# Decay weights of a graph layer: a scan along each row replaced by counts in packed bytes

## The chip, the cores and the metric

The kernel runs on one core of a Trainium2 chip. A core has five engines that run side by side and wait for one another through semaphores: TensorE (PE: matrix products, results in the memory PSUM), VectorE (DVE) and ScalarE (ACT: both work element by element on 128 partitions), GpSimd (POOL), and SyncE (SP), which here only issues transfers. Sixteen DMA engines move data between the main memory (HBM) and the core's own memory (SBUF). The metric is the time in microseconds (us) of one execution on the device.

## The reference, cut to what matters

`x` is 4096 x 64, `adj` is a 4096 x 4096 matrix of zeros and ones in fp32 (67.1 MB), and `weight` is 64 x 64.

```python
h = maximum(layernorm(x), 0)
support = h @ weight
mask = (adj != 0)
rank = cumsum(mask, axis=1)
deg = rank[:, -1:]
k = minimum(deg, 100)
pos = rank - (deg - k)
w = mask * where(pos > 0, 0.5 ** (k - pos), 0)
out = x + w @ support + bias
```

For a neighbour `j` of row `i`, let `c` be the number of neighbours of the same row that stand behind `j`. Its weight is 2 to the power of minus `c` if `c` is under 100, and 0 otherwise. A row's last neighbour has weight 1, the one ahead of it 1/2, and so on. So the work has three parts: count, along each row and from its end, the neighbours behind each column; turn the count into a power of two; and multiply the 4096 x 4096 weights by the 4096 x 64 support. TensorE sums over the partitions, so the weights must have the column `j` on the partitions, while `adj` arrives with the row `i` there: somewhere the matrix must be transposed.

## The kernel before

It takes 32 tiles of 128 rows (2 MB each). For each tile DVE makes factors `f` (1/2 at a neighbour, else 1) and runs a scan along the row from the last column to the first, which multiplies the factors up in `S`. The weight of column `j` is `S[j+1] - S[j]`. TensorE takes this difference while it transposes: two matrix products with an identity and a negative identity for each block of 128 columns. ACT copies the transposed weights from PSUM to SBUF as bf16, eight blocks to a copy. Then TensorE multiplies them by the support, which stands in three bf16 parts, 192 columns in all; ACT copies the result out, and POOL adds the three parts and the residual.

```python
apool = ctx.enter_context(tc.tile_pool(name="apool", bufs=3))      # 3 tiles of adj
work = ctx.enter_context(tc.tile_pool(name="work", bufs=2))
ps_t = ctx.enter_context(tc.tile_pool(name="ps_t", bufs=3, space=bass.MemoryType.PSUM))
ps_o = ctx.enter_context(tc.tile_pool(name="ps_o", bufs=2, space=bass.MemoryType.PSUM))
x_sb = const.tile([P, C, D], F32, name="x_sb")
nc.scalar.dma_start(x_sb, x.rearrange("(c p) d -> p c d", p=P))
# ... constants; layernorm on DVE and ACT: mean, xc, sq, var, rstd, hn ...
# ... hn transposed (line 118, fp32), times weight (line 131), cut into 3 bf16 parts: sup ...

def aggregate(po, wT, t, g):
    nonlocal osb
    for k in range(G):                                             # G = 8 blocks
        c = g * G + k
        nc.tensor.matmul(po, wT[:, c, :], sup[:, c].rearrange("p s d -> p (s d)"),   # line 148
                         start=(c == 0), stop=(c == C - 1))
    if g < NG - 1:
        return
    parts = work.tile([P, 3, D], F32, name="parts")
    nc.scalar.activation(parts, po.rearrange("p (s d) -> p s d", d=D), AF.Copy)      # 153
    # ...
    nc.gpsimd.tensor_add(parts[:, 1, :], parts[:, 1, :], parts[:, 2, :])             # 157
    nc.gpsimd.tensor_add(parts[:, 0, :], parts[:, 0, :], parts[:, 1, :])             # 158
    nc.gpsimd.tensor_add(o, parts[:, 0, :], xb[:, t, :])                             # 159
    # ... every fourth tile: nc.gpsimd.dma_start of osb ...

for t in range(C):                                                 # 32 tiles
    a_sb = apool.tile([P, N], F32, name="a_sb")
    nc.sync.dma_start(a_sb, adj[t * P:(t + 1) * P, :])
    f = work.tile([P, N], BF16, name="f")
    nc.vector.tensor_scalar(f, a_sb, 0.0, 0.5, op0=ALU.is_equal, op1=ALU.max)        # 167
    S = S_bufs[t % 2]
    nc.vector.tensor_tensor_scan(S[:, 0:N][:, ::-1], f[:, ::-1],                     # 169
                                 floor_sb.to_broadcast([P, N]), 2.0, op0=ALU.mult, op1=ALU.max)
    wT = work.tile([P, C, P], BF16, name="wT")
    po = ps_o.tile([P, 3 * D], F32, name="po")
    for g in range(NG):                                            # 4 groups of 8 blocks
        pt = ps_t.tile([P, G, P], F32, tag="pt", name=f"pt{t}_{g}")
        for k in range(G):
            j = (g * G + k) * P
            nc.tensor.matmul(pt[:, k, :], S[:, j + 1:j + 1 + P], ident_b, start=True, stop=False)  # 177
            nc.tensor.matmul(pt[:, k, :], S[:, j:j + P], nident_b, start=False, stop=True)         # 178
        nc.scalar.activation(wT[:, g * G:(g + 1) * G, :], pt, AF.Copy)               # 179
        if pending is not None:
            aggregate(*pending)
        pending = (po, wT, t, g)
```

Of the kernel before, what the change touches and what calls it, by code (L numbers as in the profile page):

```python
# [7 lines left out]

F32 = mybir.dt.float32
BF16 = mybir.dt.bfloat16  # L10
AF = mybir.ActivationFunctionType
ALU = mybir.AluOpType
AX = mybir.AxisListType

MAX_NEIGH = 100
EPS = 1e-5


@with_exitstack
def kernel(  # L20
# [5 lines left out]
    bias: bass.AP,  # L26
    out: bass.AP,
):
    """out = x + w @ (relu(layernorm(x)) @ weight) + bias.

    w[i, j] = 2^-c for a neighbour j of row i with c neighbours behind it (in the same row)
    and c < MAX_NEIGH, else 0.

    Decay weights: along each row, from the last column to the first,
        S[j] = max(f[j] * S[j+1], 2^-(MAX_NEIGH-1)),  S[N] = 2,  f = 1/2 at a neighbour, else 1.
    Then w[j] = S[j+1] - S[j]: 2^-c at a neighbour, 0 elsewhere, and 0 once S sits on its floor,
    which it reaches at the MAX_NEIGH-th neighbour from the end. All of S and w are powers of two
    (or 0), so bf16 holds them exactly. The tensor engine takes the difference while it
    transposes: wT = S[:, j+1].T @ I + S[:, j].T @ (-I).

    The fp32 support is split into three bf16 parts that sum to it exactly (8 + 8 + 8
    significant bits), so the aggregation is an fp32 product with fp32 accumulation.
    """
    nc = tc.nc
    P = 128
    N, D = x.shape
    C = N // P
    G = 8
    NG = C // G
    OG = 4  # L50

    const = ctx.enter_context(tc.tile_pool(name="const", bufs=1))
    setup = ctx.enter_context(tc.tile_pool(name="setup", bufs=1))
    apool = ctx.enter_context(tc.tile_pool(name="apool", bufs=3))
    work = ctx.enter_context(tc.tile_pool(name="work", bufs=2))
    ps_t = ctx.enter_context(tc.tile_pool(name="ps_t", bufs=3, space=bass.MemoryType.PSUM))
    ps_o = ctx.enter_context(tc.tile_pool(name="ps_o", bufs=2, space=bass.MemoryType.PSUM))

# [1 line left out]
    x_sb = const.tile([P, C, D], F32, name="x_sb")  # L60
    nc.scalar.dma_start(x_sb, x.rearrange("(c p) d -> p c d", p=P))
    w_sb = const.tile([P, D], F32, name="w_sb")
    for s in range(2):
        nc.scalar.dma_start(w_sb[s * D:(s + 1) * D, :], weight)
    bias_sb = const.tile([P, D], F32, name="bias_sb")
    nc.scalar.dma_start(bias_sb, bias.rearrange("(o d) -> o d", o=1).to_broadcast([P, D]))

# [1 line left out]
    ident = const.tile([P, P], F32, name="ident")  # L69
    make_identity(nc, ident)  # L70
    ident_b = const.tile([P, P], BF16, name="ident_b")
    nc.gpsimd.tensor_copy(ident_b, ident)
    nident_b = const.tile([P, P], BF16, name="nident_b")
    nc.gpsimd.tensor_scalar_mul(nident_b, ident, -1.0)
    floor_sb = const.tile([P, 1], F32, name="floor_sb")
    nc.gpsimd.memset(floor_sb, 2.0 ** -(MAX_NEIGH - 1))
    S_bufs = []
    for b in range(2):
        S = const.tile([P, N + 1], BF16, name=f"S{b}")
        nc.gpsimd.memset(S[:, N:N + 1], 2.0)  # L80
        S_bufs.append(S)

# [1 line left out]
    def rows(t):  # L84
        return t.unsqueeze(2).to_broadcast([P, C, D])

    mean = setup.tile([P, C], F32, name="mean")
    nc.vector.reduce_sum(mean, x_sb, axis=AX.X)  # L88
    nc.vector.tensor_scalar_mul(mean, mean, 1.0 / D)
    xc = setup.tile([P, C, D], F32, name="xc")  # L90
    nc.vector.tensor_sub(xc, x_sb, rows(mean))  # L91
    sq = setup.tile([P, C, D], F32, name="sq")
    nc.scalar.activation(sq, xc, AF.Square)  # L93
    var = setup.tile([P, C], F32, name="var")
    nc.vector.reduce_sum(var, sq, axis=AX.X)
    nc.vector.tensor_scalar(var, var, 1.0 / D, EPS, op0=ALU.mult, op1=ALU.add)
    # 1 / sqrt(var), with a Newton step for the last bits: y * (1.5 - 0.5 * var * y * y)
    rstd = setup.tile([P, C], F32, name="rstd")
    nc.scalar.activation(rstd, var, AF.Sqrt)
    nc.vector.reciprocal(rstd, rstd)  # L100
    corr = setup.tile([P, C], F32, name="corr")
    nc.vector.tensor_mul(corr, var, rstd)
    nc.vector.tensor_mul(corr, corr, rstd)
    nc.vector.tensor_scalar(corr, corr, -0.5, 1.5, op0=ALU.mult, op1=ALU.add)
    nc.vector.tensor_mul(rstd, rstd, corr)
    hn = setup.tile([P, C, D], F32, name="hn")
    nc.vector.tensor_mul(hn, xc, rows(rstd))  # L107

    xb = const.tile([P, C, D], F32, name="xb")
    nc.gpsimd.tensor_add(xb, x_sb, bias_sb.unsqueeze(1).to_broadcast([P, C, D]))  # L110

# [1 line left out]
    hT = setup.tile([P, C // 2, P], F32, name="hT")  # L113
    for g in range(C // 2 // G):
        pt = ps_t.tile([P, G, P], F32, tag="pt", name=f"pth{g}")
        for k in range(G):
            a = g * G + k
            nc.tensor.transpose(pt[:, k, :], hn[:, 2 * a:2 * a + 2, :].rearrange("p c d -> p (c d)"), ident)  # L118
        nc.scalar.activation(hT[:, g * G:(g + 1) * G, :], pt, AF.Relu)  # L119

    sup = const.tile([P, C, 3, D], BF16, name="sup")
    CS = G * P // D
    for g in range(C // CS):
        pt = ps_t.tile([P, G, P], F32, tag="pt", name=f"pts{g}")
        # the two row halves of hT go to one bank each
        pv = pt.rearrange("p (s h) (q d) -> p s (h q) d", s=2, d=D)
        part = sup[:, g * CS:(g + 1) * CS].rearrange("p (k s) e d -> p s k e d", s=2)
        for k in range(CS // 2):
            a = g * (CS // 2) + k
            for s in range(2):  # L130
                nc.tensor.matmul(pv[:, s, k, :], hT[s * D:(s + 1) * D, a, :], w_sb[s * D:(s + 1) * D, :],  # L131
                                 start=True, stop=True)
        rest = setup.tile([P, 2, CS // 2, D], F32, name="rest", bufs=2)
        nc.scalar.activation(part[:, :, :, 0, :], pv, AF.Copy)  # L134
        nc.vector.tensor_sub(rest, pv, part[:, :, :, 0, :])  # L135
        nc.scalar.activation(part[:, :, :, 1, :], rest, AF.Copy)
        nc.vector.tensor_sub(part[:, :, :, 2, :], rest, part[:, :, :, 1, :])

# [1 line left out]
    out_t = out.rearrange("(c p) d -> p c d", p=P)  # L140
    osb = None
    pending = None

    def aggregate(po, wT, t, g):
        nonlocal osb
        for k in range(G):
            c = g * G + k
            nc.tensor.matmul(po, wT[:, c, :], sup[:, c].rearrange("p s d -> p (s d)"),  # L148
                             start=(c == 0), stop=(c == C - 1))
        if g < NG - 1:  # L150
            return
        parts = work.tile([P, 3, D], F32, name="parts")
        nc.scalar.activation(parts, po.rearrange("p (s d) -> p s d", d=D), AF.Copy)  # L153
        if t % OG == 0:
            osb = work.tile([P, OG, D], F32, name="osb")
        o = osb[:, t % OG, :]
        nc.gpsimd.tensor_add(parts[:, 1, :], parts[:, 1, :], parts[:, 2, :])  # L157
        nc.gpsimd.tensor_add(parts[:, 0, :], parts[:, 0, :], parts[:, 1, :])  # L158
        nc.gpsimd.tensor_add(o, parts[:, 0, :], xb[:, t, :])  # L159
        if t % OG == OG - 1:  # L160
            nc.gpsimd.dma_start(out_t[:, t - OG + 1:t + 1, :], osb)  # L161

    for t in range(C):
        a_sb = apool.tile([P, N], F32, name="a_sb")
        nc.sync.dma_start(a_sb, adj[t * P:(t + 1) * P, :])
        f = work.tile([P, N], BF16, name="f")
        nc.vector.tensor_scalar(f, a_sb, 0.0, 0.5, op0=ALU.is_equal, op1=ALU.max)  # L167
        S = S_bufs[t % 2]
        nc.vector.tensor_tensor_scan(S[:, 0:N][:, ::-1], f[:, ::-1], floor_sb.to_broadcast([P, N]), 2.0,  # L169
                                     op0=ALU.mult, op1=ALU.max)  # L170
        wT = work.tile([P, C, P], BF16, name="wT")
        po = ps_o.tile([P, 3 * D], F32, name="po")
        for g in range(NG):
            pt = ps_t.tile([P, G, P], F32, tag="pt", name=f"pt{t}_{g}")
            for k in range(G):
                j = (g * G + k) * P
                nc.tensor.matmul(pt[:, k, :], S[:, j + 1:j + 1 + P], ident_b, start=True, stop=False)  # L177
                nc.tensor.matmul(pt[:, k, :], S[:, j:j + P], nident_b, start=False, stop=True)  # L178
            nc.scalar.activation(wT[:, g * G:(g + 1) * G, :], pt, AF.Copy)  # L179
            if pending is not None:  # L180
                aggregate(*pending)
            pending = (po, wT, t, g)
    aggregate(*pending)


# [26 lines left out]
```

## Time and profile before

| | |
|---|---|
| time, median of 3 runs | 440.5 us (437.2 to 440.66) |
| span of the profiled run | 435.5 us |
| busy: DVE, POOL, PE, ACT | 370.5, 331.3, 255.4, 148.8 us |
| read from HBM | 68.22 MB, a mean of 159 GB/s over the span |
| mean granted TensorE clock | 0.863 of full speed |

Busy times of different engines overlap, so they do not add up to the span. A row of the profile's groups gives the line of the kernel, the engine, the operation, the written and the read tile with their shapes, the count, the busy time, the mean duration of one in ns, and the idle time of the engine just before them with what ended it. The chain of work that ended last is followed back from the last instruction, at each step to what released it; POOL leads it here, and an engine that leads it can itself be held up by another, so it has to be read together with the order of time. In the table of stretches the columns are the stretch in us, its length, the busy time of PE, PEld (the loads of the fixed operand), DVE, ACT and POOL with the number of instructions in brackets, the granted TensorE clock, the busy share of the DMA engines and their GB/s.

### The profile page before, as it was taken

What the parts mean: (1) busy time and instruction counts of PE and PEld (TensorE: products, weight loads), DVE (VectorE), ACT (ScalarE), POOL (GpSimd) and SP (SyncE); (2) the same over time, 40 slices, a digit from 0 to 9 for tenths busy, and PEclk for the clock granted to TensorE, in tenths of its full rate; (3) what the DMA queues carried; (4) which work ended last, traced back from release to release, by engine and by line L of the source; (5) the groups of instructions that cost most, each with busy time, mean ns of one, the idle gap of its engine ahead of it and who ended that gap; (6) DMA issues with size and microseconds to landing.
All of it is one profiled execution on the core that took longest, in us unless ns stands there. A gap on an engine that the chain in (4) does not pass through costs nothing.

```text
span 435.5 us, 6885 instructions
## 1 busy us (share of the span) xinstructions
PE 255.4 (59%) x3152; PEld 245.7 (56%) x3152; DVE 370.5 (85%) x79; ACT 148.8 (34%) x171; POOL 331.3 (76%) x116
## 2 busy tenths in 40 slices
PE   0000029857749666877748549578387569585394
PEld 0000028857639556766648549567387568585383
DVE  0089974999997997999979998999989979999570
ACT  0011107534415405434225314344064036251253
POOL 1040000699999997999999996999999969999752
PEclk9999999988887968888669788987888869698798
DMA  8914850055555555355553455555554553300000
GB/s 322 350 32 170 337 206 36 2 194 194 193 194 206 193 194 190 111 184 196 181 191 148 182 193 206 194 193 194 194 206 172 191 188 102 135 2 2 12 2 12
DMA packets 6365, 69.70 MB, mean 160 GB/s; under 512 B 961, under 2 KB 1985, under 8 KB 2241
## 3 DMA queue, kind: packets, MB, share of 16 engines
q1 hardware_dynamic: 4608, 67.11, 42.1%
q10 hardware_dynamic: 1344, 1.11, 1.1%
q0 software_dynamic: 384, 1.05, 0.7%
q8 instruction: 24, 0.39, 0.4%
q14 instruction: 5, 0.03, 0.0%
HBM read 68.22 MB, written 1.05 MB: 159 GB/s over the span
## 4 chain that ended last, share of the span: by engine, by line
POOL 69%; PE 8%; DVE 7%; issue 5%; DMA 5%; ACT 4%; POOLq 0%; ACTq 0%
POOL osb L159 26%; POOL parts L157 23%; POOL parts L158 20%; DMA x_sb<-in_x_dram 5%; PE po L148 3%; DVE f L167 3%; ACT wT L179 2%; DVE S L169 2%; PE pt L177 2%; PE pt L178 2%; PE pts L131 1%; PE pth L118 1%; ACT parts L153 1%; POOL out_dram L161 1%; DVE hn L107 1%
## 5 line engine op out<-in xcount | busy, mean ns | idle before, releaser
L169 DVE TENSOR_TENSOR_SCAN S<-f,floor_sb 128x4096 bf16<-128x4096 bf16 x32 | 280.9, 8779 | 19.3 <-PE pt L178 19.3
L177 PE MATMUL pt<-ident_b,S 128*128 128x128 bf16 x1024 | 152.9, 242 | 64.8 <-DVE S L169 64.3
L179 ACT ACTIVATE wT<-pt 128x1024 bf16<-128x1024 f32 x128 | 130.1, 1024 | 156.0 <-PE pt L178 156.0
L157 POOL TENSOR_TENSOR parts<-parts 128x64 f32<-128x64 f32 x32 | 114.6, 3581 | 71.0 <-ACT parts L153 70.9
L178 PE MATMUL pt<-nident_b,S 128*128 128x128 bf16 x1024 | 152.4, 241 | 0.0
L177 PEld LDWEIGHTS <-S 128*128 128x128 bf16 x1024 | 112.8, 111 | 69.8 <-DVE S L169 69.5
L148 PE MATMUL po<-sup,wT 128*128 128x192 bf16 x1024 | 124.9, 274 | 46.4 <-ACT wT L179 46.3
L148 PEld LDWEIGHTS <-wT 128*128 128x128 bf16 x1024 | 97.9, 110 | 49.8 <-ACT wT L179 48.0
L159 POOL TENSOR_TENSOR osb<-parts,xb 128x64 f32<-128x64 f32 x32 | 115.0, 3595 | 2.5
L178 PEld LDWEIGHTS <-S 128*128 128x128 bf16 x1024 | 113.0, 110 | 0.8 <-issue 0.6
L158 POOL TENSOR_TENSOR parts<-parts 128x64 f32<-128x64 f32 x32 | 90.1, 2815 | 2.5
L167 DVE TENSOR_SCALAR f<-a_sb 128x4096 bf16<-128x4096 f32 x32 | 76.8, 2402 | 1.0
L118 PE MATMUL pth<-ident,hn 128*128 128x128 f32 x16 | 3.6, 423 | 63.1 <-DVE hn L107 63.1
L118 PEld LDWEIGHTS pth<-ident,hn 128*128 128x128 f32 x16 | 3.3, 227 | 63.0 <-issue 63.0
L153 ACT ACTIVATE parts<-po 128x192 f32<-128x192 f32 x32 | 10.5, 329 | 62.4 <-POOL osb L159 59.6
L88 DVE TENSOR_REDUCE mean<-x_sb 128x32 f32<-128x2048 f32 x1 | 2.3, 2286 | 22.9 <-DMA x_sb<-in_x_dram 22.9
L110 POOL TENSOR_TENSOR xb<-x_sb,bias_sb 128x2048 f32<-128x2048 f32 x1 | 4.5, 4495 | 22.1 <-DMA bias_sb<-in_L_gnn_bias_dram 22.1
L135 DVE TENSOR_TENSOR rest<-pts,sup 128x1024 f32<-128x1024 f32 x2 | 2.5, 1226 | 7.6 <-ACT sup L134 7.6
L93 ACT ACT_TABLE_LOAD x1 | 1.3, 1283 | 21.0 <-issue 21.0
L93 ACT ACTIVATE sq<-xc 128x2048 f32<-128x2048 f32 x1 | 1.9, 1909 | 18.9 <-DVE xc L91 18.9
L161 POOL DMA_DIRECT2D out_dram<-osb x8 | 6.3, 792 | 2.4 <-POOL osb L159 2.4
L119 ACT ACTIVATE hT<-pth 128x1024 f32<-128x1024 f32 x2 | 2.0, 1024 | 8.3 <-PE pth L118 8.3
(28 smaller groups left out, 26.3 us busy)
## 6 DMA issues: line engine op xcount, KB each, us to landing
a_sb<-in_adj_dram SPq DMA_DIRECT2D x32, 2048.0 KB, 8.0
out_dram<-osb POOLq DMA_DIRECT2D x8, 128.0 KB, 6.1
w_sb<-in_L_gnn_weight_dram ACTq DMA_DIRECT2D x2, 16.0 KB, 12.1
bias_sb<-in_L_gnn_bias_dram ACTq DMA_DIRECT2D x1, 32.0 KB, 3.0
x_sb<-in_x_dram ACTq DMA_DIRECT2D x1, 0.2 KB, 22.2
```

The source lines that it names most:

```text
L118: nc.tensor.transpose(pt[:, k, :], hn[:, 2 * a:2 * a + 2, :].rearrange("p c d -> p (c d)"), ident)
L148: nc.tensor.matmul(po, wT[:, c, :], sup[:, c].rearrange("p s d -> p (s d)"), start=(c == 0), stop=(c == C - 1))
L153: nc.scalar.activation(parts, po.rearrange("p (s d) -> p s d", d=D), AF.Copy)
L157: nc.gpsimd.tensor_add(parts[:, 1, :], parts[:, 1, :], parts[:, 2, :])
L158: nc.gpsimd.tensor_add(parts[:, 0, :], parts[:, 0, :], parts[:, 1, :])
L159: nc.gpsimd.tensor_add(o, parts[:, 0, :], xb[:, t, :])
L161: nc.gpsimd.dma_start(out_t[:, t - OG + 1:t + 1, :], osb)
L167: nc.vector.tensor_scalar(f, a_sb, 0.0, 0.5, op0=ALU.is_equal, op1=ALU.max)
L169: nc.vector.tensor_tensor_scan(S[:, 0:N][:, ::-1], f[:, ::-1], floor_sb.to_broadcast([P, N]), 2.0, op0=ALU.mult, op1=ALU.max)
L177: nc.tensor.matmul(pt[:, k, :], S[:, j + 1:j + 1 + P], ident_b, start=True, stop=False)
L178: nc.tensor.matmul(pt[:, k, :], S[:, j:j + P], nident_b, start=False, stop=True)
L179: nc.scalar.activation(wT[:, g * G:(g + 1) * G, :], pt, AF.Copy)
```

## The change

It is a new formulation of the whole kernel. Its steps:

1. Rows are taken in 8 chunks of 512, and columns in 2 halves, the right half first: 16 units, each of 4 loaded tiles of 128 rows x 2048 columns (1 MB). The tile buffers become 8 of 1 MB instead of 3 of 2 MB. Within a unit, partition `p` of a tile holds one of 16 rows that lie next to one another, so a tile's 128 runs of 8 KB lie 256 KB apart in HBM.
2. `convert`: DVE (in three of the 64 tiles ACT, by the sign) writes a byte for each element, 64, or 65 at a neighbour. Four columns, 512 apart, share one 32-bit word.
3. `transpose`: TensorE transposes such words as fp32 numbers, four columns in each pass, 4 blocks to a tile; `settle` (DVE) copies them out. Read as fp16, a word is two numbers, each with two masks in it: a step of its low byte and a step of its high byte are two fixed steps of its value.
4. `totals`, `split`, `suffix`, `clamp`: products with band matrices sum up each run of 32 columns, ACT reads the sums as bytes from PSUM, a product with `later` adds up what lies behind each run, and DVE cuts that at 100.
5. `scan`: for each 128 fp16 numbers, one product with a triangular matrix counts within the runs and a second adds what lies behind. The constants are such that the fp32 sum in PSUM has the two counts in its two lowest bytes.
6. `weigh`: ACT reads those bytes straight from PSUM and writes 2 to the power of minus the count, 128 x 1024 elements to an instruction.
7. `aggregate`: the normalised `x`, in two parts, is the fixed operand, and the weights are streamed 512 at a time. The product with `weight` comes after the sum, once for each chunk (`project`).
8. All these tasks are put in one fixed order by a list in the program, and the engines are held to it. Extra products on an unused tile keep TensorE busy in the first stretch. Two tiles of `adj` are loaded ahead of `x`, and the last chunk is drained, projected and stored in two halves.

What it is for: to take the serial scan off DVE, to transpose four columns with each pass, and to have no engine wait long for another. The core of the diff, cut (the constants, the layernorm and its own transposes are left out, and the list is shortened):

```diff
-    apool = ctx.enter_context(tc.tile_pool(name="apool", bufs=3))
-    work = ctx.enter_context(tc.tile_pool(name="work", bufs=2))
-    ps_t = ctx.enter_context(tc.tile_pool(name="ps_t", bufs=3, space=bass.MemoryType.PSUM))
-    ps_o = ctx.enter_context(tc.tile_pool(name="ps_o", bufs=2, space=bass.MemoryType.PSUM))
+    apool = ctx.enter_context(tc.tile_pool(name="apool", bufs=NA))          # NA = 8
+    bpool = ctx.enter_context(tc.tile_pool(name="bpool", bufs=6))
+    mpool = ctx.enter_context(tc.tile_pool(name="mpool", bufs=3))
+    wpool = ctx.enter_context(tc.tile_pool(name="wpool", bufs=NP + 4))      # NP = 8
+    ps_t = ctx.enter_context(tc.tile_pool(name="ps_t", bufs=2, space=bass.MemoryType.PSUM))
+    ps_v = ctx.enter_context(tc.tile_pool(name="ps_v", bufs=4, space=bass.MemoryType.PSUM))
...
-        nc.vector.tensor_scalar(f, a_sb, 0.0, 0.5, op0=ALU.is_equal, op1=ALU.max)
-        nc.vector.tensor_tensor_scan(S[:, 0:N][:, ::-1], f[:, ::-1], floor_sb.to_broadcast([P, N]), 2.0,
-                                     op0=ALU.mult, op1=ALU.max)
...
+    def convert(n):
+        m8 = bpool.tile([P, Q, E], U8, name="m8")                           # Q = 512, E = 4
+        m_v, a_v = m8.rearrange("p q e -> p e q"), tiles.pop(n).rearrange("p (e q) -> p e q", e=E)
+        if n in signed:                                                     # (4, 8, 11)
+            nc.scalar.activation(m_v.bitcast(I8), a_v, AF.Sign)
+        else:
+            nc.vector.tensor_scalar(m_v, a_v, 0.0, 64.0, op0=ALU.not_equal, op1=ALU.add)
...
+        for c in range(c0, c1):                                             # transpose: 4 to a tile
+            nc.tensor.transpose(pts[u, tt][:, c, :], m32[:, c * P:(c + 1) * P], ident)
...
+            nc.vector.tensor_copy(mw, pt)                                   # settle: 128 x 512 words
...
+        for e in range(E // 2):                                             # totals: 8 to a unit
+            for c in range(CB):
+                nc.tensor.matmul(tot[SUB * c:SUB * (c + 1), :], band[:, at:at + SUB], masks[u][:, c, :, e], ...)
...
+    def split(u):
+        nc.scalar.activation(sums8[u], tots[0].bitcast(U8).rearrange("p (i f) -> p f i", f=4)[:, 1:3, :], AF.Copy)
...
+        for f in range(2):                                                  # suffix
+            nc.tensor.matmul(px, later[:, 1 - u % H, f, :], sums[:, f, :], start=(f == 0), stop=(f == 1))
...
+        nc.vector.tensor_scalar(behind[u], ..., excess[:, h:h + 1], float(MAX_NEIGH), op0=ALU.subtract, op1=ALU.min)
...
+    def scan(u, k):                                                         # 8 to a unit
+        v = vs[u, k] = ps_v.tile([P, W], F32, tag="v", name="v")            # W = 512 rows
+        nc.tensor.matmul(v, tri, masks[u][:, k % CB, :, k // CB], start=True, stop=False)
+        nc.tensor.matmul(v, where[:, k, :], behind[u], start=False, stop=True)
+
+    def weigh(u, k):
+        wts[u, k] = wpool.tile([P, 2, W], F32R, name="wk")
+        v = vs.pop((u, k)).bitcast(U8).rearrange("p (i f) -> p f i", f=4)[:, :2, :]
+        nc.scalar.activation(wts[u, k], v, AF.Exp, scale=-LN2, bias=floor)
+
+    def aggregate(u, k):
...
+        for s in range(2):
+            nc.tensor.matmul(accs[0], hr[:, h * HB + k // CB * 2 * CB + s * CB + k % CB, :, :].rearrange("p s d -> p (s d)"), wk[:, s, :],
+                             start=((h, k, s) == (1, 0, 0)), stop=((h, k, s) == (0, NP - 1, 1)))
...
+    def drain(g, part=None):                                                # ACT; the last half DVE
+    def project(g, part=None):                                              # PE: 4 fp32 products, 64 columns
+    def finish(g, part=None):                                               # DVE add, then the store
...
+    places = {"v": 4, "t": 2, "b": 6, "w": NP + 4}                          # the list: next task by rank
+    while kinds:                                                            # and by when it may start
...
+            if end is not None and at - end > 700:
+                warm((at - end) // 430)                                     # extra products on TensorE
...
+    for i in nc.cur_bb.bb.instructions:                                     # PE, DVE, ACT, POOL:
+            if i.engine in last:                                            # held to program order
+                tc.add_manual_dep(i, last[i.engine], ..., reason="program order")
```

## The prediction, made before the changed kernel ran

> **What bounds the kernel now.** I read the costliest groups first, then the chain that ended last, then the order of time of single engines, then the table of stretches. The groups:
>
> ```profile
> L169 DVE TENSOR_TENSOR_SCAN S<-f,floor_sb 128x4096 bf16<-128x4096 bf16 x32 | 280.9, 8779 | 19.3 <-PE pt L178 19.3
> L179 ACT ACTIVATE wT<-pt 128x1024 bf16<-128x1024 f32 x128 | 130.1, 1024 | 156.0 <-PE pt L178 156.0
> L159 POOL TENSOR_TENSOR osb<-parts,xb 128x64 f32<-128x64 f32 x32 | 115.0, 3595 | 2.5
> L167 DVE TENSOR_SCALAR f<-a_sb 128x4096 bf16<-128x4096 f32 x32 | 76.8, 2402 | 1.0
> ```
>
> DVE needs a scan and a conversion for each tile, 8.78 + 2.40 = 11.2 us, and has almost no idle time ahead of the two (19.3 + 1.0 us in all). The chain gives POOL 69%, but the order of time of POOL shows the same 64-element addition in two durations:
>
> ```profile
> 145.60 8.70 POOL L157 TENSOR_TENSOR parts<-parts 128x64 f32<-128x64 f32 x1
> ...
> 167.82 0.32 POOL L158 TENSOR_TENSOR parts<-parts 128x64 f32<-128x64 f32 x1
> ```
>
> It takes 0.32 us by itself, and 8.7 us while a DVE scan runs (from 145.38, for 8.81 us). POOL is held up by DVE and now and then hands a delay of 2.3 us on. DVE is the bound: 32 x 11.2 = 358 us, 20 us of stalls, about 31 us before the first scan at 31.05 and 13.5 us after the last. That leaves some 13 us of the 435.5 for the layernorm's pieces on DVE. PE idles in each tile, and the stretches show what that costs it and what the transfers can do:
>
> ```profile
> 127.00:128.00 1.00, 0.00 (x0) 0.00 (x0) 1.00 (x1) 0.00 (x0) 1.00 (x1) 1.00 0.69 279
> ...
> 129.00:130.00 1.00, 0.00 (x0) 0.00 (x0) 0.97 (x2) 0.21 (x1) 1.00 (x2) 0.50 0.00 0
> ```
>
> ```profile
> 47.00:55.00 8.00, 0.00 (x0) 0.00 (x0) 8.00 (x2) 0.00 (x0) 0.00 (x0) 1.00 1.01 432
> ...
> 88.00:400.00 312.00, 211.18 (x2579) 203.35 (x2577) 297.37 (x55) 116.54 (x134) 297.60 (x84) 0.83 0.47 172
> ```
>
> PE's last product before the pause starts at 124.12; by 129 the granted clock is half. Transfers reach 432 GB/s where a buffer is free, and 172 on average, as they wait for DVE. Two rows give PE's rate at full and half clock, by the distance of starts (0.05 to 0.06 and 0.10 to 0.11 us for 128 columns):
>
> ```profile
> 122.12 0.22 PE L178 MATMUL pt<-nident_b,S 128*128 128x128 bf16 x1
> 122.17 0.22 PE L177 MATMUL pt<-ident_b,S 128*128 128x128 bf16 x1
> ...
> 132.99 0.31 PE L177 MATMUL pt<-ident_b,S 128*128 128x128 bf16 x1
> 133.09 0.31 PE L178 MATMUL pt<-nident_b,S 128*128 128x128 bf16 x1
> ```
>
> **What the Trainium skill says.** "TensorE: Matmul & The Clock Gate", Part 1: the clock is halved after an idle window of about 3.4 us and given back after as long a busy one. The trace agrees (idle from 124.3, half clock before 129). "ScalarE: Activation LUTs", What ACT_TABLE_LOAD costs: any function costs one element a cycle at 1.2 GHz, a per-partition bias adds about 93 ns, neighbours overlap by as much. The trace has two copies of 128x1024 in 1.93 us at 130.02, so 0.92 us from start to start; no Exp with a bias runs here. "VectorE: DVE Perf Modes", Mode 2x_2P: a tensor-with-scalar operation from SBUF to SBUF handles two fp32 elements a cycle. L167 agrees (4096 in 2.29 us alone, 1787 a microsecond), but no byte output runs here. The first page's Part 3 says that products into different strips of 32 output rows run side by side, 2.38 times as fast for three; no run here shows it.
>
> **The change, part by part.** Removed: all 281 us of scans, half-clock waits, POOL's additions in the loop. Added, engine by engine, over 16 units of 4 MB:
>
> *DMA.* 68.2 MB / 432 GB/s = 158 us, ready at about 161 with the start. The 256 KB distance between runs is new; I assume the same rate.
>
> *DVE.* A conversion has half L167's elements. Of L167's 2.29 us alone, 4096 elements at two a cycle of 0.96 GHz (that page's clock) are 2.13 and 0.16 is fixed; 2048 take 1.07 + 0.16 = 1.23 us, and 61 of them 75 us. Settle copies 512 words from PSUM; L135 does 1024 in 1226 ns, so about 0.65 us, times 64 = 42 us. Clamps 16 x 0.65 = 10. Layernorm and setup about 15. Sum 142 us.
>
> *ACT.* Weigh: 0.92 us, plus 0.09 us for its bias, = 1.01; x 128 = 129 us. Split 16 x 0.92 = 15. Seven drains of 512 elements: 0.92 - 512 x 0.00083 = 0.49, so 3.5. Three conversions at 1.9 (L93's 2048 elements take 1909 ns) = 6. Layernorm pieces and x's own copies about 10, a table load 1.3 (as at L93). Sum 165 us.
>
> *PE* at full clock. 128 columns take 55 ns and eight products of 192 start 0.66 us ahead of the next work, 82 ns each; the slope is 0.42 ns a column, so 512 columns take 0.217 us. Scan and aggregate are four such products for each of the 128 steps: 0.868 x 128 = 111 us. This assumes that the fp32r weights stream at bf16's rate. Transposes: L118 shows 16 fp32 blocks in 3.65 us, 0.228 each, right after 63 us of idle PE. The record there says clock 1.00, but I take it as the half clock by the page above, so 0.114 warm; 256 x 0.114 = 29. Totals 16 x 0.5 (side by side) = 8; suffix 16 x 0.43 = 7; project 8 x 0.9 (fp32, small, estimated from L131's 62 ns for half as deep a product, with a load each) = 7. Sum 162 us, plus extra warming products early, which cost nothing.
>
> So for each unit of 4 tiles DMA needs 9.8 us, PE 10.1, ACT 9.6 and DVE 8.3: four engines nearly equal, where before one had 11.2 us for each half as large a tile (22.4 for the same 4 MB).
>
> *On the path.* Two tiles and x are 3.1 MB, 7.3 us, landed by about 11 us with some 3 us of start and latency (as 2 MB took 7.6 us to land, 4.85 of them at the full rate); tiles three and four land by 16. Then convert 1.2, transpose 0.5, settle 0.65, totals 0.6, split 1.0, suffix 0.45, clamp 0.65, scan 0.45 and about eight hand-overs of 0.15 us: the first weigh at about 23 us. After it ACT still has about 152 us and PE about 157 (a few transposes and one unit's totals are done). The end behind the last weigh: aggregate 0.45, drain 0.4, project 0.5, finish 0.3, store about 3: 5 us. PE: 23 + 157 + 5 = 185; ACT: 180; DMA: 161 + the last unit's chain of 7 us + 8 weighs of 1.01 + 5 = 181. With four streams this close, a fixed order and 2 to 4 buffers between them, none runs without gaps. I add 4% of the 157 us, 6 us: a span of 191. The times before lie 1.7 to 5.2 us above the profiled span, so 193 us for the median.
>
> **The rivals.** (1) *DVE becomes the bound*: if a byte output 4 bytes apart lifts the conversion out of the doubled rate, it takes 2.29 us (as DVE's 2048-element fp32 additions do, L107), DVE has 207 us and the time is near 235. Against it, L167's output is 16-bit beside a 32-bit input and runs doubled, so the output's width alone doesn't stop it. 8%. (2) *The clock falls*: with the mean 0.83 of before PE's 157 us become 189, the time 225. Against it: gaps of over 3.4 us caused that clock, and the new order leaves none in steady flow. A few such gaps would cost 2 us each. 7%. (3) *fp32r at half rate or transposes at 0.228 us*: 55 or 29 us more on PE, 220 to 250. L118 leaves the second open. 8%. (4) *Transfers bound*: at 380 GB/s for scattered runs 68.2 MB take 180 us and the time is 203. The rate of 403 GB/s in the first 11 us of before, with small packets between, speaks against much worse. 20%. (5) *The four fit together almost without gaps*: 184 us. 20%.
>
> **Range and chances.** The centre is 193. Case 5 gives the low end, case 4 and a larger loss by waiting (10% of 157) the high end: 182 to 212. Each of cases 1 to 3 lies above it, though they are the less likely; all of them still lie at half the time before. Slower than 431 us would take an error of two in the bound's sum. So 0.98 for faster.
>
> **What would show each step right or wrong.** Weigh near 1.0 us from start to start, x128, with ACT busy over 80% from 25 us on. Convert near 1230 ns and settle near 650; a mean of 2300 means rival 1. Granted clock over 0.95 after 25 us; 512-column products 0.22 us apart; transposes 0.11 us apart. GB/s near 400 in steady flow, with loads that wait for a free buffer rather than tiles that wait for a load. The first weigh at 22 to 25 us. A tail of 5 us behind the last weigh. The prediction is wrong if one of these unit costs is off by 10%, as that engine then sets the pace for all 16 units.

## The result, and the profile after

The changed kernel takes 210.05 us (median of 5 runs, 209.83 to 211.0) against 440.5 us before: a ratio of 0.479, 95% interval 0.477 to 0.481. The profiled span is 209.0 us. The first lines are the busy time of each engine and the chain that ended last, from the page of the changed kernel:

```profile
PE 194.1 (93%) x1089; PEld 112.6 (54%) x1089; DVE 152.2 (73%) x184; ACT 174.3 (83%) x172; POOL 30.8 (15%) x43
...
DMA 36%; PE 35%; DVE 18%; ACT 4%; POOL 3%; issue 1%; DVEq 0%; POOLq 0%; ACTq 0%
```

Four streams are close to one another, as the change intended, and the chain names two of them, DMA and PE, with equal shares. The groups that took the place of the scan, the transposes and the copies:

```profile
L328 ACT ACTIVATE wk<-v,floor 128x1024 fp32r<-128x1024 uint8 x128 | 139.1, 1118 | 13.8 <-PE v L323 10.7
L273 DVE TENSOR_SCALAR m<-a_sb 128x2048 uint8<-128x2048 f32 x61 | 87.9, 1445 | 12.4 <-DMA a_sb<-in_adj_dram 12.2
L336 PE MATMUL acc<-wk,hr 128*128 128x512 f32 x256 | 91.4, 444 | 1.6 <-DVE hr L262 0.9
L283 PE MATMUL pt<-ident,m 128*128 128x128 f32 x256 | 47.5, 276 | 5.1 <-DVE m L273 4.2
L292 DVE COPY mt<-pt 128x512 uint32<-128x512 uint32 x61 | 41.6, 685 | 13.6 <-PE pt L283 13.4
L322 PE MATMUL v<-mt,tri 128*128 128x512 f16 x128 | 50.7, 396 | 0.4 <-ACT wk L328 0.4
```

The 281 us of scans are gone. No PE group of these has more than 5.1 us of idle time ahead of it, where line 177 (the first product of each transpose) had 64.8 before:

```profile
L177 PE MATMUL pt<-ident_b,S 128*128 128x128 bf16 x1024 | 152.9, 242 | 64.8 <-DVE S L169 64.3 <-DVE rest L135 0.5
```

The stretches (columns as before) show where each engine stands in steady flow, and that the start and the end are different:

```profile
25.00:40.00 15.00, 11.80 (x61) 5.82 (x60) 14.05 (x17) 13.77 (x13) 6.73 (x2) 1.00 1.02 422
...
100.00:120.00 20.00, 19.63 (x115) 10.91 (x113) 17.98 (x20) 17.74 (x18) 1.30 (x2) 1.00 1.01 421
...
180.00:200.00 20.00, 19.87 (x103) 10.94 (x101) 3.51 (x6) 19.20 (x20) 0.56 (x1) 1.00 0.02 7
200.00:209.00 9.00, 4.04 (x14) 2.55 (x14) 0.91 (x3) 2.32 (x3) 0.00 (x0) 0.71 0.05 15
```

In steady flow PE is busy for 98% of the time at full clock, and the transfers run at 421 GB/s without a break. The last load lands at 169.7 us, 39 us ahead of the end. A busy PE can hide waits, since the ends of its products are modelled; so I took the distances from start to start. One step of the changed kernel, from PE's order of time (start, duration, both in us):

```profile
148.03 0.71 PE L336 MATMUL acc<-wk,hr 128*128 128x512 f32 x2
148.58 0.40 PE L322 MATMUL v<-mt,tri 128*128 128x512 f16 x1
148.81 0.38 PE L323 MATMUL v<-behind,where 128*128 128x512 f16 x1
149.03 0.38 PE L283 MATMUL pt<-ident,m 128*128 128x128 f32 x2
149.17 0.71 PE L336 MATMUL acc<-wk,hr 128*128 128x512 f32 x2
```

The aggregate's pair takes 0.55 us, the two scan products 0.23 and 0.22, two transposes 0.14: 1.14 us to the next step. I sorted the distances from 46 to 178 us by the product and its two neighbours; what lies above the lower quartile of each sort comes to some 4.5 of 132 us. So PE works almost without gaps. The instants of the 16 splits give the length of a unit: from the third at 45.7 to the fifteenth at 177.5 us, 10.98 us each, where I had 10.1 for PE without waits. (A split is the one instruction in each unit in which ACT reads the sums of the runs.)

### The profile page after: what moved, and what is told of

The parts are those of the page before. It is cut to its first block, busy times and chain, and to the rows that moved or that the text cites. A ratio compares the mean times of both kernels' runs of the same rounds, so it can differ in the third digit from the quotient of the medians.

```text
span 209.0 us, 2957 instructions
## 1 busy us (share of the span) xinstructions
PE 194.1 (93%) x1089; PEld 112.6 (54%) x1089; DVE 152.2 (73%) x184; ACT 174.3 (83%) x172; POOL 30.8 (15%) x43
## 4 chain that ended last, share of the span: by engine, by line
DMA 36%; PE 35%; DVE 18%; ACT 4%; POOL 3%; issue 1%; DVEq 0%; POOLq 0%; ACTq 0%
DMA a_sb<-in_adj_dram 36%; PE acc L336 12%; DVE m L273 8%; PE v L322 6%; PE v L323 5%; PE pt L283 5%; DVE mt L292 3%; PE po L359 2%; ACT wk L328 2%; PE tot L302 2%; ACT xt L221 2%; POOL rstd L252 2%; PE pc L227 2%; PE ps L313 1%; DVE var L250 1%
## 5 line engine op out<-in xcount | busy, mean ns | idle before, releaser
L328 ACT ACTIVATE wk<-v,floor 128x1024 fp32r<-128x1024 uint8 x128 | 139.1, 1118 | 13.8 <-PE v L323 10.7
L273 DVE TENSOR_SCALAR m<-a_sb 128x2048 uint8<-128x2048 f32 x61 | 87.9, 1445 | 12.4 <-DMA a_sb<-in_adj_dram 12.2
L336 PE MATMUL acc<-wk,hr 128*128 128x512 f32 x256 | 91.4, 444 | 1.6 <-DVE hr L262 0.9
L283 PE MATMUL pt<-ident,m 128*128 128x128 f32 x256 | 47.5, 276 | 5.1 <-DVE m L273 4.2
L292 DVE COPY mt<-pt 128x512 uint32<-128x512 uint32 x61 | 41.6, 685 | 13.6 <-PE pt L283 13.4
L322 PE MATMUL v<-mt,tri 128*128 128x512 f16 x128 | 50.7, 396 | 0.4 <-ACT wk L328 0.4
L283 PEld LDWEIGHTS pt<-ident,m 128*128 128x128 f32 x256 | 34.3, 141 | 29.3 <-issue 5.6
L323 PE MATMUL v<-behind,where 128*128 128x512 f16 x128 | 48.3, 377 | 0.0
L336 PEld LDWEIGHTS acc<-wk,hr 128*128 128x128 f32 x256 | 40.5, 190 | 11.3 <-issue 3.6
L307 ACT ACTIVATE sums<-tot 128x1024 f16<-128x1024 uint8 x16 | 16.5, 1029 | 0.2 <-PE tot L302 0.2
L209 PE MATMUL none<-junk 128*128 128x512 bf16 x31 | 10.8, 492 | 1.3 <-DVE junk L126 1.3
L302 PE MATMUL tot<-mt,band 128*32 128x512 f16 x128 | 10.2, 392 | 1.5 <-DVE mt L292 1.2
L341 POOL TENSOR_TENSOR xr<-xr,bias_sb 128x256 f32<-128x256 f32 x8 | 8.6, 1073 | 10.2 <-DMA bias_sb<-in_L_gnn_bias_dram 10.0
## 6 DMA issues: line engine op xcount, KB each, us to landing
w_sb<-in_L_gnn_weight_dram SPq DMA_DIRECT2D x2, 16.0 KB, 16.5
```

The costliest lines, as they stand in the source:

```text
L273: nc.vector.tensor_scalar(m_v, a_v, 0.0, 64.0, op0=ALU.not_equal, op1=ALU.add)
L283: nc.tensor.transpose(pts[u, tt][:, c, :], m32[:, c * P:(c + 1) * P], ident)
L292: nc.vector.tensor_copy(mw, pt)
L302: nc.tensor.matmul(tot[SUB * c:SUB * (c + 1), :], band[:, at:at + SUB], masks[u][:, c, :, e], start=(h == 1 and e == 0), stop=(e == 1), sk ...
L307: nc.scalar.activation(sums8[u], tots[0].bitcast(U8).rearrange("p (i f) -> p f i", f=4)[:, 1:3, :], AF.Copy)
L322: nc.tensor.matmul(v, tri, masks[u][:, k % CB, :, k // CB], start=True, stop=False)
```

## The experiments

**What sets the pace.** Three kernels each take away part of what one theory holds for the bound: PE's products, ACT's elements, or the loads.

One aggregate product for each step:

```diff
-        for s in range(2):
+        for s in range(1):
             nc.tensor.matmul(accs[0], hr[...], wk[:, s, :],
-                             start=((h, k, s) == (1, 0, 0)), stop=((h, k, s) == (0, NP - 1, 1)))
+                             start=((h, k, s) == (1, 0, 0)), stop=((h, k, s) == (0, NP - 1, 0)))
```

> The aggregate makes one product for each step in place of two (the second half of the weights is computed but left out of the sum, so the output lacks part of the sum). Theory 1, PE sets the pace: a step of 1.147 us loses at least one 512-column product of 0.23 to 0.28 us, PE then needs about 8.7 us for a unit, less than the transfers (10.0) and ACT (9.3), and the time falls from 210 to 187-195 us. Theory 2, ACT sets the pace (busy 174 of 209 us): within 3 us of 210. Theory 3, the transfers set the pace (36% of the chain): within 3 us of 210.

Measured 206.96 us (206.62 to 207.4), so theory 1 as I had put it missed: about 30 us of products (128 at 0.23) were taken away, and 3 us came back.

Half of each weigh:

```diff
-        nc.scalar.activation(wts[u, k], v, AF.Exp, scale=-LN2, bias=floor)
+        nc.scalar.activation(wts[u, k][:, :1, :], v[:, :1, :], AF.Exp, scale=-LN2, bias=floor)
...
-            nc.tensor.matmul(accs[0], hr[...], wk[:, s, :], ...)
+            nc.tensor.matmul(accs[0], hr[...], wk[:, 0, :], ...)
```

> Each weigh handles only the first 512 of its 1024 elements, and both aggregate products stream that half (the second half of the weights is left out, the number of products is unchanged). ACT loses about 128 x 0.43 = 55 us. Theory 1, PE sets the pace: steps stay at 1.147 us and only the last six, where PE waits for ACT, shorten: 204-209 us. Theory 2, ACT sets the pace: under 185 us. Theory 3, transfers: within 3 us of 210.

Measured 208.14 us (208.07 to 208.63). ACT's busy time from 46 to 178 us falls from 120 to 82 us, and PE keeps 131 of 132. ACT does not set the pace, and the step of PE stays at 1.14 to 1.15 us, so the 0.55 of its pair holds no wait for ACT.

Half of the loads:

```diff
+        if n % 2:
+            tiles[n] = pairs[n - 1]
+            return
-        tiles[n] = apool.tile([P, N // H], F32, tag="a_sb", name="a_sb")
+        pairs[n] = tiles[n] = apool.tile([P, N // H], F32, tag="a_sb", name="a_sb")
```

> Every second tile is not loaded: its conversion reads the tile ahead of it again (half of adj is left out; all other work is unchanged). Bytes read fall from 68 to 35 MB. Theory 1, PE sets the pace: 205-210 us, at most the start gets shorter. Theory 3, the transfers set the pace in the middle, as the chain says: under 195 us. Theory 2, ACT: as theory 1.

Measured 211.59 us (211.02 to 211.87): the transfers alone do not set it either, though the chain of the changed kernel gave them 36%. The time lies 1.5 us above the changed kernel and above all three ranges; in the profile the first weigh comes at 28.8 us, 1.3 us later than there (see "The start"). With half of them gone the chain of this kernel reads:

```profile
PE 79%; DVE 11%; POOL 4%; ACT 2%; issue 2%; DVEq 0%; POOLq 0%; ACTq 0%
```

Each wait for a transfer had another stream of nearly the same pace behind it, and the chain can show only one of the two. DVE's order of time in the kernel with one aggregate product shows what holds that one:

```profile
90.21 0.68 DVE L292 COPY mt<-pt 128x512 uint32<-128x512 uint32 x1
91.43 1.38 DVE L273 TENSOR_SCALAR m<-a_sb 128x2048 uint8<-128x2048 f32 x1 [0.54 <-DMA a_sb<-in_adj_dram]
92.70 0.67 DVE L292 COPY mt<-pt 128x512 uint32<-128x512 uint32 x1
93.91 1.39 DVE L273 TENSOR_SCALAR m<-a_sb 128x2048 uint8<-128x2048 f32 x1 [0.54 <-DMA a_sb<-in_adj_dram]
95.19 0.74 DVE L318 TENSOR_SCALAR behind<-ps,excess 128x512 f16<-128x512 f32 x1
```

A conversion starts every 2.49 us, the time of 1 MB at 421 GB/s, and waits for its load. Settles and clamps, whose data are ready, stand behind it in DVE's fixed order, and PE and ACT wait for them. The settle at 90.21, for instance, copies what PE had transposed by 88.9; PE's totals wait for it, and ACT's split for the totals:

```profile
90.94 0.64 PE L302 MATMUL tot<-mt,band 128*32 128x512 f16 x8 [1.34 <-DVE mt L292]
```

```profile
91.62 1.02 ACT L307 ACTIVATE sums<-tot 128x1024 f16<-128x1024 uint8 x1 [0.64 <-PE tot L302]
```

From 46 to 166 us PE waits 10.8 us in this way for settles ahead of its totals. In DVE's order there are five conversions, not four, between some clamps (6, 2, 5, 5, 4, 4, 5, 4, 4, 4, 5, 4, 4, 3, 2, 0 ahead of the 16 clamps). It was laid out by the list for PE's planned pace, which is slower than that of the loads. So a faster PE stays held to the order made for the slower one. Two more runs test that (theory 4).

Both cuts at once, with the two diffs above:

> Both cuts at once: one aggregate product for each step, and every second tile not loaded (both leave part of the computation out). Each alone left the time at 207 and 211.6 us. Theory 4: two bounds lie at nearly the same pace, PE's steps (1.147 us, 10.7 us a unit) and DVE's fixed order, in which conversions wait for loads at 2.49 us a tile with a settle or clamp behind them, four or five to a unit. Then neither cut alone helps and both together do: ACT is left as the bound, about 9.4 us a unit, and the time is 183-192 us. Rival: something else has that pace, such as ACT with its hand-overs at each unit, or the order itself: 204-208 us.

Measured 197.95 us (196.89 to 198.04). One cut alone gave -3 us, the other +1.5; both give -12. This is more than their sum, but short of the 183 to 192 that I expected. A unit takes 9.9 us from the third split (47.3) to the fifteenth (166.0), and ACT is busy 126 of the 132 us from 46 to 178. So its own work is 9.4 us a unit, as expected; what I had left out is 0.5 us of waits a unit, as PE (123 of 132) and DVE (112) are nearly as busy. That ACT is the bound here is likely, but no run of its own shows it.

One aggregate product, all loads, and the list told of it (the planned hold is the time in ns for which the list takes an engine as occupied by a task; it shapes the order and is no wait in the program):

```diff
-            task(aggregate, (u, k), PE, 8 * u + k + 3, 460, 700, [("weigh", u, k), ...
+            task(aggregate, (u, k), PE, 8 * u + k + 3, 240, 480, [("weigh", u, k), ...
```

> One aggregate product for each step (part of the sum is left out), all loads kept, and the list told so: the aggregate's planned hold is 240 ns in place of 460, which lays out the order anew (clamps come after about four conversions each, the last one behind the last conversion, where the old order leaves one or two units for after it). Theory 4: the pace is that of the loads, 10.0 us a unit, and what is left behind the last load shrinks from 37 us to 20-24: 189-196 us. Rival, the order doesn't matter: within 3 us of the 207 of the same cut in the old order.

Measured 195.23 us (194.77 to 195.68), 12 us less than the same computation in the old order. The conversions ahead of the clamps are now 6, 2, 4, 5, 3, 5, 4, 3, 4, 3, 4, 5, 4, 4, 3, 2; added up, 39 conversions stand ahead of the tenth clamp where 43 stood in the old order. Four loads are 10 us, and the tenth clamp comes at 116.5 us in place of 126.3. The last clamp runs at 176.6 us in place of 186.3, and a unit takes 9.8 us. The loads come at 10.0 us a unit, and ACT is busy 128 of 132 us: both are near their limit.

The same number in the list of the changed kernel itself, which keeps both products:

> The changed kernel, computation complete and unchanged (fp32r, two aggregate products), with nothing but the list's planned hold of the aggregate at 240 ns in place of 460, so another fixed order. If PE sets the pace of the changed kernel (no idle time from 46 to 178 us, 10.7 us a unit), another order cannot gain: 206-212 us. If the order alone was what held it, as the same order brought the kernel with one aggregate product from 207 to 195: under 203 us.

Measured 209.31 us (208.96 to 209.38); the changed kernel, run beside it:

> The changed kernel itself, on the same chip as the three runs beside it: 209-211.5 us.

gave 210.02 us (209.68 to 210.38). So this other order is worth 0.7 us here, and 12 with one product less: the order is not what holds the changed kernel, PE is. The loads through DVE's order are a second bound that shows only when PE is relieved.

**What a step of PE is made of.** The weights and the operand as bf16 in place of fp32r (the 32-bit type in which the changed kernel gives them to PE), the computation complete:

```diff
-    hr = const.tile([P, B, 2, D], F32R, name="hr")
+    hr = const.tile([P, B, 2, D], BF16, name="hr")
...
-        nc.vector.tensor_sub(hr[:, own(h), 1, :], xs[:, own(h), :], hr[:, own(h), 0, :].bitcast(F32))
+        nc.vector.tensor_sub(hr[:, own(h), 1, :], xs[:, own(h), :], hr[:, own(h), 0, :])
...
-        wts[u, k] = wpool.tile([P, 2, W], F32R, name="wk")
+        wts[u, k] = wpool.tile([P, 2, W], BF16, name="wk")
```

> The weights and the two parts of the normalised x are bf16 in place of fp32r (the powers of two stay exact, x keeps 16 significant bits in its two parts). Theory A, what the aggregate costs over 0.217 us a product is the loading of its 32-bit fixed operand (190 ns, against 97 to 100 for the 16-bit ones): the pair falls from 0.555 to 0.43-0.46 us behind transposes, a step to 1.02-1.06 us, and the time to 193-201 us, where ACT (1.0 us a step) and the transfers (10.0 us a unit) take over. Theory B, it is the fp32 transposes ahead of it that must finish, whatever the operand's type: the pair stays at 0.53 us or more and the time within 3 us of 210.

Measured 207.45 us (207.15 to 207.78), and the step, from PE's order of time in this kernel:

```profile
148.10 0.38 PE L283 MATMUL pt<-ident,m 128*128 128x128 f32 x2
148.32 0.59 PE L336 MATMUL acc<-wk,hr 128*128 128x512 bf16 x2
148.75 0.39 PE L322 MATMUL v<-mt,tri 128*128 128x512 f16 x1
148.98 0.38 PE L323 MATMUL v<-behind,where 128*128 128x512 f16 x1
149.19 0.38 PE L283 MATMUL pt<-ident,m 128*128 128x128 f32 x2
```

The pair falls to 0.43 us, as theory A has it, but two transposes now take 0.22 instead of 0.14. So 0.08 us of the pair's fall is only a matter of where the records put the start of the pair; transposes and pair together fall from 0.69 to 0.65. The step is 1.09 us where A expected 1.02 to 1.06, and the time stays above A's range; DVE still has the old order. Without transposes between, pair and scan take 0.91 to 0.93 us with fp32r and 0.87 with bf16 (both near the end, where no transposes are left), so theory B, which puts it all down to the transposes, is out. Whether the 0.05 us left is the load of the 32-bit operand alone was not tried apart: from start to start the pair's second product takes 0.24 us with fp32r and 0.216 with bf16.

The same with the list's hold at 430 ns:

> The complete computation with bf16 weights and operand, and the aggregate's planned hold at 430 ns. Theory 4: the old order held bf16's 1.09 us steps to PE's old pace; with the new one a unit takes 10.2 us of PE, and the time falls from 207.5 to 199-204 us. Rival: within 1.5 us of 207.5.

Measured 205.12 us (204.81 to 205.5), 2.3 us less; below the old order, above the expected range. Of the 2.2 us between the two profiles 1.1 stand ahead of the first weigh (27.7 us in place of 28.8; see "The start"), so the order is worth about 1 us here. With the hold at 240 ns, as above:

> The complete computation with bf16 weights and operand in that same order (planned hold 240 ns). PE needs 8 x 1.09 + 1.45 = 10.2 us a unit, so from the first scan at 27 us 16 units end at 190, and with the end's 7 us and 2 us from span to time: 198-203 us, if PE sets the pace. If the order of the bf16 kernel before (205) was not what held it: 204-206 us.

Measured 203.22 us (203.17 to 203.88), 0.2 us above the expected range. A unit takes 10.6 us where I had 10.2: that sum has no waits in it, and 0.4 us a unit are left over, as in the changed kernel. Against the fp32r kernel in the same order (209.31) this is 6.1 us less, and 128 steps with 0.05 us less each are 6.4. So the time follows PE's step.

**The end.** Extra products to keep the clock up:

```diff
+        if f is aggregate and args[0] == U - 1 and args[1] > NP - 4 or f is project and args[0] == U // 2 - 1:
+            keep(2 if f is aggregate else 3)      # products of an unused tile
```

> As the bf16 kernel with its new list, and two extra products on an unused tile ahead of each of the last three aggregates and three ahead of each half of the last projection. Theory: TensorE's clock halves at the end (0.50 from 204 us) as it waits for ACT, and the eight small products of the last projection take 1.9 us instead of 0.9; with the clock kept up the time falls by 0.7-1.2 us against the kernel without them. Rival: those products are slow for another reason, or the extra ones stand in their way: no change or slower by up to 1 us.

Measured 205.75 us (205.49 to 205.95), no gain over 205.12. The two halves of the last projection in this kernel:

```profile
198.73 0.66 PE L367 MATMUL po<-w_sb,acc_sb 128*128 128x64 f32 x4 [0.35 <-ACT acc_sb L361]
199.23 0.81 PE L217 MATMUL spare<-junk 128*128 128x512 bf16 x3
199.88 0.55 PE L367 MATMUL po<-w_sb,acc_sb 128*128 128x64 f32 x4
```

The clock stays at 1.00 and a half takes 0.55 to 0.66 us, but the three extra products between the halves take 0.65 us (199.23 to 199.88). From the first to the last product the projection lasts 1.70 us, and 1.58 in the kernel without them. In the changed kernel the eight products took 1.87 us at half clock in one profile and 1.26 in the other. The first weigh of this kernel comes at 28.5 us against 27.7 without the products (see "The start"), which is more than the 0.6 us by which it is slower.

**The start.** The layernorm's products on PE put behind the first unit's transposes:

```diff
-    xt = apool.tile([P, N // H], F32, tag="a_sb", name="xt")
+    xt = setup.tile([P, N // H], F32, name="xt")
...
-        task(center, (b0,), PE, -10, 880, 1070, [("turned", 1, HT - 4)], ("v", ("centered", b0)))
-        task(centered, (b0,), ACT, -11, 560, 680, [("center", b0)])
-    task(count, (), PE, -9, 120, 300, [("center", HB - 4)], ("v", ("counted",)))
+        task(center, (b0,), PE, -5, 880, 1070, [("turned", 1, HT - 4)], ("v", ("centered", b0)))
+        task(centered, (b0,), ACT, -5, 560, 680, [("center", b0)])
+    task(count, (), PE, -16, 120, 300, [("turned", 1, HT - 4)], ("v", ("counted",)))
```

> As the bf16 kernel with the hold of 240 ns, and x's second step at the start (32 fp32 products on PE, 3.8 us) put behind the first unit's transposes by its rank, with a buffer of its own for the transposed x. If the first weigh is late (27.5 us, predicted 23) because the first unit's transposes and totals stand behind these products in PE's order, it comes 1 to 2 us sooner, and the time falls by 0.5 to 2 us against the kernel without this. Otherwise no change.

Measured 201.32 us (201.07 to 202.97); ratio to before 0.460 (0.456 to 0.463). The first weigh comes at 26.4 us instead of 27.7, and the time is 1.9 us lower. This complete computation is the best of the runs, 8.7 us under the changed kernel run beside it.

The first weigh also moves without any edit. The changed kernel, then the bf16 kernel, which have the same order up to there:

```profile
12.50:15.00 2.50, 2.50 (x24) 2.46 (x23) 1.47 (x2) 1.91 (x4) 0.00 (x0) 0.96 1.00 419
```

```profile
12.50:15.00 2.50, 2.50 (x14) 2.07 (x13) 1.44 (x2) 1.19 (x3) 0.00 (x0) 0.50 1.02 429
```

In spite of the extra products the granted clock falls to half in the first stretch, at 8 to 11 us. Where it is back at full speed by 14.5 us (eight of the twelve profiles without this edit), the first weigh comes at 27.5 to 27.8 us; where it takes until 15 or 16 us (the other four), at 28.5 to 28.8. So 1 us between two kernels can come from there alone. The 26.4 us of this edit lie below both groups.

## Why the prediction held in its range and missed its centre

The range of 182 to 212 us holds 210; the centre of 193 is 17 us short. That the range held is in part luck: its high end stood for transfers at 380 GB/s and for waits of 10%, and neither came (421 GB/s, waits of 3%). The mechanism was right: the scan goes, and PE, first by a little among four streams, sets the pace. The sizes add up as follows, on the span (191 predicted, 209.0 measured).

*The unit of PE, +8 us.* I had 10.1 us and, apart from it, 6 us of waits in all (0.4 a unit); it is 10.98 with waits. The waits were about right (4.5 us in 132, so 0.38 a unit). The term "128 x 0.868 plus transposes at 0.114" was mis-sized: the step is 1.14 to 1.15 us instead of 1.096. The scan's products take 0.23 and 0.22 instead of 0.217, and the fp32r pair with its two transposes 0.69 instead of 0.66. The assumption that fp32r costs no more than bf16 is what failed, by 0.05 us a step; with bf16 the pair (0.43) and the transposes (0.11 each) are as worked out, and the step is 1.09. Rival 3 is out: at half rate a pair would take 0.87 us. Totals took 0.57 us a unit against 0.5. Over 16 units (10.98 - 10.13) x 16 = 13.6 us, of which 6 were allowed for.

*The first weigh, +4.5 us.* I summed the first unit's chain as if its engines were free and came to 23 us; it starts at 27.46. These lines of DVE and PE in the changed kernel show why:

```profile
16.58 0.69 DVE L292 COPY mt<-pt 128x512 uint32<-128x512 uint32 x1 [1.96 <-PE pt L283]
17.19 1.37 DVE L273 TENSOR_SCALAR m<-a_sb 128x2048 uint8<-128x2048 f32 x1
...
21.57 1.28 DVE L292 COPY mt<-pt 128x512 uint32<-128x512 uint32 x2
...
26.04 0.73 DVE L318 TENSOR_SCALAR behind<-ps,excess 128x512 f16<-128x512 f32 x1
```

```profile
17.33 3.81 PE L227 MATMUL pc<-less,xt 128*128 128x128 f32 x32
20.98 0.38 PE L283 MATMUL pt<-ident,m 128*128 128x128 f32 x2
...
21.25 0.64 PE L283 MATMUL pt<-ident,m 128*128 128x128 f32 x4
```

The first unit's last tile lands at 15.7 us, but its conversion stands behind a settle that waits for PE, and is done by 18.6; its transposes stand behind 3.8 us of the layernorm's products in PE's order and start at 21.25. The first clamp likewise stands behind a conversion on DVE until 26.04. Moving those products won 1.3 us of it; the rest, the stretch at half clock among it, was not tried apart.

*The end, +4 us.* After PE's last scan product (start 199.01) ACT still weighs what stands in the four PSUM buffers, until 201.93; I had let the last weigh end with PE's work. Behind it come 7.0 us, not 5: the last projection alone took 1.9 us at a clock of 0.50 where I had 0.5. The three parts give 16.5 of the 18 us.

*Other engines.* Weigh was right: three in 3.12 us, 1.0 apart. The conversion keeps the doubled rate with byte output (1.29 us at least, 1.39 in the median, predicted 1.23), so rival 1 is out. With 1.39 it is 13% off all the same, and DVE did not become the bound: the sign "off by 10%" was too strict for an engine with room to spare. Settle took 0.685 us (0.65). The transfers ran at 421 GB/s, not 432, with runs 256 KB apart, and ended at 169.7 us, not 161. The sign for them failed: tiles wait for loads (12.2 us ahead of the conversions), not loads for buffers. The 403 GB/s that I gave for the first 11 us of before hold from 3 to 11 us; over all 11 it is 320. The clock was 1.00 from 25 to 200 us, so rival 2 is out. Rival 4 had slower transfers, which did not come; that the loads hold DVE's order costs 12 us, but only in the kernel with one aggregate product. Rival 5, a fit almost without gaps, would have needed the predicted step, start and end as well.

*What I had not seen.* I treated the four streams as independent and added a share for waits. The runs show that the fixed order ties them: what a faster engine wins is lost at a conversion that waits for its load with ready work behind it, until the order is laid out anew.

The Trainium skill's "TensorE: Matmul & The Clock Gate", Part 3, said that products into different strips run side by side; the eight of totals take 0.57 us, where eight one after another would take 1.74 at 0.217, so the measurement agrees.

## What to carry to other kernels

When several engines need nearly the same time, cut one at a time and then two together: a cut without effect can mean two equal bounds rather than a wrong suspect, and the chain of waits then names only one of them. In a program held to a fixed order, change the plan behind the order along with the work; here the same cut was worth 3 us in the old order and 15 in a new one. Sum the first unit's chain with what stands ahead of each task in its engine's queue, and the last unit's with the buffers still to be emptied.

## What the runs showed of the hardware

- An aggregate pair of 512-column products with fp32r operands takes 0.55 us behind two fp32 transposes (0.14), with bf16 operands 0.43 behind 0.22: together 0.69 and 0.65. Without transposes between, pair and scan together take 0.93 us at the end of the changed kernel (starts at 196.28 and 197.21) and 0.87 at the end of the bf16 kernel with the hold of 240 ns (189.69 and 190.56).
- ACT reads every fourth byte of PSUM at about the rate of a plain copy: 1.0 us for 1024 elements, start to start, with a bias; the fp32 copies of before take 0.92 without one.
- A power of 128x16 elements on POOL takes 2.9 and 3.8 us (L252), some ten times the 0.32 us of an addition of 128x64 there.
